# Softmax sums of the first batch moved from TensorE to GpSimd and VectorE, weight tiles moved by SyncE's queue, opening loads on two queues

## The chip, the cores and the metric

The kernel runs on one core of one Trainium2 chip. The metric is the device time of one launch in microseconds, as the median of the runs shown. A core has TensorE (PE in the profile; its weight loads are PEld), VectorE (DVE), ScalarE (ACT), GpSimd (POOL) and SyncE (SP), each with a queue of its own that it works off in order, and 16 DMA engines that all queues share. Matrix products land in PSUM, everything else lives in SBUF.

## The reference

The input x has 4 batches of 512 rows of 512. Post-norm attention with 16 query heads of 32 and a single key and value head, then a gated feed-forward part whose weights are quantized to -1, 0 and 1.

```python
q = rotary((x @ Wq + bq) split into 16 heads of 32)
k = rotary(x @ Wk + bk); v = x @ Wv + bv          # one head, shared by all
attn = softmax(q k^T / sqrt(32), axis=-1)
x = layernorm(x + (attn v) @ Wo + bo)

quantize(w) = clip(round(w / (mean(abs(w)) + 1e-8)), -1, 1)
h = sigmoid(x @ quantize(w1).T) * (x @ quantize(w2).T)   # 512 -> 1408
out = layernorm(x + h @ quantize(w3).T)
```

All data are float32. w1, w2 and w3 have 1408 x 512 elements each.

## The kernel before

**Steps.** The heads are handled in 4 chunks c of 4 heads (4 x 32 partitions), the keys in 4 tiles t of 128. The main loop runs over 64 steps (b, c, t); here step 0 to step 15 are batch 0. In step n the kernel issues, in this order on each engine: `scores` (products `ps`, in two PSUM pairs j of two heads each, less the row maxima `negm` by a product with ones; then two exponentials `es` of 128 x 1024 on ScalarE); `weigh` of the step before (products `acc` of `es` and v); `find_maxima` for step n + 7 (products `pmax`, again two pairs, and two maxima reductions `mx` on VectorE); one `quantize` job; some filler work; another `quantize` job in batch 0; and twice, in the middle and at its end, `due()`, which counts a slot and runs one piece of each entry in `late` whose slot has come.

**PSUM.** The pool `ps_sc` has two buffers of two banks, tag `sc`. `ps` and `pmax` take turns in them, so `pmax` waits for the exponentials of the same step, and the `ps` of the next step waits for the maxima of this one. `acc` and `den` have one bank each, and `ps_mm` two banks for the filler.

**Filler.** `project_in` makes k, v and the queries of a batch (`pk`, `pq`, then a rotation on VectorE of four operations: `a`, a shuffle, one with `sin_sb`, the addition; if it runs before step 0, ScalarE first copies the product to `r`). `project_out` and `feed_forward` follow for batches that are done. `fill.draw(pace)` takes so many microseconds of it in a step by lengths written into the code. In batch 0 the filler is the projection of batches 1 and 2.

**Maxima.** After the fourth `t` of a chunk, `spread` transposes the maxima on PE (`pm`, between the two groups of `pmax`), makes two rows of them (`m`), and sends them by SyncE to DRAM (`rows`) and back (`negm`). For batches 1 to 3 the queries are split in two parts (`halves`: a copy on ScalarE, a subtraction on GpSimd), stored (`qw`, `qp`) and loaded per head (`qr`), three steps ahead. From step 9 on, `pmax` is of that kind (kr, qr).

**Softmax sums.** In batch 0, `count` multiplies each `es` by ones on PE into the PSUM tile `den` (4 products of 512 columns, each in two passes). At the end of a chunk `normalize` copies `den` to SBUF on ScalarE, sends one row of every four heads to DRAM and back as 128 x 16 (`few`), takes the reciprocal, and loads it spread over the partitions (`rden`); GpSimd multiplies `ctxT` by it. In batches 1 to 3 GpSimd adds the `es` of the four t into `total` (four additions of 128 x 512 a step from t = 1 on), and `normalize` reduces `total` on VectorE with 32 x 32 transposes (`part`, two instructions), goes through DRAM (`parts`) to a `few` of 32 x 4 x 64, and reduces, inverts and transposes that (three instructions).

**Quantizing.** `quantized` works in 66 jobs: 33 first passes (ScalarE sums absolute values, `junk`) and 33 second ones (ScalarE's `sgn`, VectorE's `raw`, then a store to DRAM as `w`). A raw tile is loaded four jobs ahead into one of nine buffers and stored two jobs after it is done. In `now > PER` (after step 16) `sgn` is put in PSUM, before that in SBUF. Both transfers are issued by GpSimd:

```python
pool.dma_start(out=raws[k], in_=wf[m, f])       # load(k), line 178
pool.dma_start(out=w.bitcast(F32), in_=q)       # the store, line 218
```

All other transfers go through `move`, line 83, on SyncE, in the order in which the program issues them.

**Opening.** SyncE loads `bkv`, `bq`, `wkv`, the four x-transposed tiles of batch 0 (`xT`), and then the query weights and rotary tables. PE meanwhile runs 24 products of ones (`WARM`, 48 passes of 128 columns), then `pk`, which needs `wkv` and the four `xT`. Before step 0 the kernel finds the maxima of steps 0 to 6.

Helpers record all engine instructions under line 75, products under 80, transposes on PE under 86 and SyncE's transfers under 83, so the profile is read by tile names.

Of the kernel before, what the change touches and what calls it, by code (L numbers as in the profile page):

```python
# [28 lines left out]
def postln_block(  # L29
# [20 lines left out]
    NG = P // HD  # L50
    SCALE = 1.0 / float(HD) ** 0.5
    W = 512
    WARM = 24

    const = ctx.enter_context(tc.tile_pool(name="const", bufs=1))
    small = ctx.enter_context(tc.tile_pool(name="small", bufs=2))
# [25 lines left out]
    def move(out, in_):  # L82
        pin(nc.sync.dma_start(out=out, in_=in_))  # L83
# [34 lines left out]

    chunks = iter([(b, c) for b in range(B) for c in range(NC)])

    def load_xT(n):

        for _ in range(n):
            b, c = next(chunks, (None, None))
            if b is not None:
                batches[b].xT.append(work.tile([P, T], F32, tag="xT", name="xT", bufs=6))
                move(batches[b].xT[c], xT[b, :, c, :])

    move(bkv_sb, bkv)
    move(bq_sb, bq)  # L130
    move(wkv_sb, wkv)
    load_xT(NC)
    move(wq_sb[0], wq[:, 0])
    move(cos_sb, cos)
    move(sin_sb, sin)
# [22 lines left out]
    def quantized():  # L158

        order = ((0, False), (1, False), (0, True), (2, False), (1, True), (2, True))
        jobs = [(m, last, f) for m, last in order for f in range(NF)]

        means = {}
        for n, (m, last) in enumerate(order):
            if not last:
                for k, step in ((2, 0), (6, 1), (10, 2)):
                    means[(n + 1) * NF + k] = (m, step)
        raws, part, row, pg, hi, waiting = {}, {}, {}, {}, {}, []  # L170

        def load(k):
            if k < len(jobs):
                m, _, f = jobs[k]

                tag, bufs = ("wd", 5) if k % 2 else ("wg", 4)
                raws[k] = wp.tile([P, W], F32, tag=tag, name="raw", bufs=bufs)
                pool.dma_start(out=raws[k], in_=wf[m, f])

        def mean(m, step):  # L180
            if step == 0:
                row[m] = small.tile([P, 1], F32, tag="row", name="row")
                dve.tensor_reduce(row[m], part[m], AX.X, ALU.add)
            elif step == 1:
                pg[m] = ps_mm.tile([P, 1], F32, tag="mm", name="pg")
                mm(pg[m], ones, row[m], True, True)
                gamma = small.tile([P, 1], F32, tag="gamma", name="gamma")
                act.activation(gamma, pg[m], AF.Identity, scale=1.0 / (NF * W * P), bias=eps_q)
                row[m] = gamma
            else:  # L190
                hi[m] = small.tile([P, 1], F32, tag="hi", name="hi")
                act.mul(hi[m], row[m], 0.5)

        AHEAD = 4
        for k in range(AHEAD):
            load(k)
        for k, (m, last, f) in enumerate(jobs):
            load(k + AHEAD)
            if k in means:
                mean(*means[k])  # L200
            raw = raws.pop(k)
            if not last:
                if f == 0:
                    part[m] = small.tile([P, NF], F32, tag="part", name="part", bufs=3)
                junk = work.tile([P, W], BF16, tag="th", name="junk")
                act.activation(junk, raw, AF.Abs, accum_out=part[m][:, f : f + 1])
            else:
                if now > PER:

                    sgn = ps_acc.tile([P, W], F32, tag="den", name="sgn")  # L210
                else:
                    sgn = work.tile([P, W], BF16, tag="th", name="sgn")
                act.activation(sgn, raw, AF.Sign, bias=hi[m])
                dve.scalar_tensor_tensor(raw, raw, hi[m], sgn, ALU.is_gt, ALU.min)
                waiting.append((kept[m][f], raw))
            if len(waiting) > 2 or k + 1 == len(jobs):
                for w, q in waiting[: 1 if k + 1 < len(jobs) else 3]:
                    pool.dma_start(out=w.bitcast(F32), in_=q)
                del waiting[:1]
            yield  # L220

# [182 lines left out]
    def scores(b, c, t):  # L404
        s = batches[b]
        pss = []
        for j in range(2):
            ps = ps_sc.tile([P, 2, T], F32, tag="sc", name="ps")
            pss.append(ps)
            for i in range(2):  # L410
                rows = ts(2 * j + i, HD)
                mm(ps[:, i, :], s.kT[rows, ts(t, P)], s.q[c][rows, :], True, False)
        for j, ps in enumerate(pss):
            for i in range(2):
                rows = slice(HD * (2 * j + i), HD * (2 * j + i) + 2)
                mm(ps[:, i, :], ones_r[rows, :], s.negm[c][rows, :], False, True)
        es = []
        for j, ps in enumerate(pss):
            e = esp.tile([P, 2, T], F32, tag="es", name="es")
            act.activation(e, ps, AF.Exp, scale=SCALE)  # L420
            es.append(e)
        if b > 0:

            if t == 0:
                s.first = es
            elif t == 1:
                s.total = [work.tile([P, 2, T], F32, tag=f"total{j}", name="total", bufs=1) for j in range(2)]
                for j in range(2):
                    for i in range(2):
                        pool.tensor_tensor(  # L430
                            s.total[j][:, i, :], s.first[j][:, i, :], es[j][:, i, :], ALU.add
                        )
            else:
                for j in range(2):
                    for i in range(2):
                        pool.tensor_tensor(
                            s.total[j][:, i, :], s.total[j][:, i, :], es[j][:, i, :], ALU.add
                        )
        return es

    def columns(out, left, right, start, stop):
# [9 lines left out]
        if t == NT - 1:  # L451
            act.copy(s.ctxT[c], s.acc)

    def count(b, c, t, es):

        s = batches[b]
        if t == 0:
            s.den = ps_acc.tile([P, T], F32, tag="den", name="den")
        columns(s.den, ones[:, 0:HD], es, t == 0, t == NT - 1)

    def normalize(b, c):

        s = batches[b]
        flat = dram.tile([NG, T], F32, tag="flat1", name="flat", bufs=3)
        if b > 0:

            n = T // HD
            part = work.tile([P, NG * n], F32, tag="sums", name="part", bufs=1)
            for j in range(2):
                dve.tensor_reduce(  # L470
                    part[:, ts(j, 2 * n)],
                    s.total[j].rearrange("p i (a r) -> p (i a) r", r=HD),
                    AX.X, ALU.add, apply_transpose=True,
                )
                if j == 0 and c + 1 < NC:
                    yield
            yield
            parts = dram.tile([P // HD, HD, NG * n], F32, tag="parts", name="parts", bufs=3)
            move(parts.rearrange("o r k -> (o r) k"), part)
            yield  # L480
            few = work.tile([HD, P // HD + 2, NG * n], F32, tag="rot_b", name="few", bufs=1)
            move(few[:, 0 : P // HD, :], parts.rearrange("o r k -> r o k"))
            yield
            if c + 1 < NC:
                yield
            whole, lines = few[:, P // HD, :], few[:, P // HD + 1, :]
            dve.tensor_reduce(whole, few[:, 0 : P // HD, :].rearrange("r o k -> r k o"), AX.X, ALU.add)
            dve.reciprocal(whole, whole)
            dve.transpose(lines, whole)
            move(  # L490
                flat.rearrange("(b h) (a r) -> (h a) b r", b=2, r=HD),
                lines.rearrange("x (b r) -> x b r", b=2),
            )
        else:
            sums = work.tile([P, T], F32, tag="sums", name="sums", bufs=1)
            act.copy(sums, s.den)
            yield
            sent = dram.tile([NG, T], F32, tag="flat0", name="sent", bufs=3)
            move(sent, sums.rearrange("(i r) k -> i r k", r=HD)[:, 0])
            yield  # L500
            few = small.tile([P, NG * T // P], F32, tag="few", name="few")
            move(few, sent.rearrange("i (r j) -> (i r) j", r=HD))
            yield

            if c + 1 < NC:
                yield
            dve.reciprocal(few, few)
            move(flat.rearrange("i (r j) -> (i r) j", r=HD), few)
        yield
        rden = work.tile([P, T], F32, tag="rden", name="rden", bufs=1)  # L510
        for i in range(NG):
# [343 lines left out]
    for n, (b, c, t) in enumerate(steps):  # L855
# [4 lines left out]
        es = scores(b, c, t)  # L860
        if last is not None:
            weigh(*last)
        if last is not None and last[0] == 0:
            count(*last)
        last = (b, c, t, es)
        if n == NC * NT // 2:

            late.append((slot, load_x(0)))
        if t == NT - 1:
            begin = slot + 3  # L870
            late.append((begin, normalize(b, c)))
            if c == NC - 1:
                late.append((begin + 7, feed(b)))
# [91 lines left out]
```

## Time and profile before

| | us |
|---|---|
| runs | 670.32, 671.13, 673.02 (median 671.13) |
| profiled execution | 672.56 |
| its span, from the first to the last instruction | 670.8 |
| PE / VectorE / ScalarE / GpSimd busy | 644.7 / 430.0 / 282.8 / 324.4 |
| start of the first product `pk` | 9.77 |
| first `ps`, step 0 | 48.2 |
| batch 0, to its last `pq` | 48.2 to 161.3 |

The profile is that of one execution. "Busy" of PE counts overlapping passes once and includes passes that wait, so it is no measure of work. Views used below: the page (busy times, 40 slices of the span with a digit for the busy tenths, the chain of waits, groups of instructions), the stretches (busy time of every engine between two times), the answer for one tile, and the timeline (start, duration, engine, line, operation, out<-in, shape, count, and in brackets the idle time before it and what ended it). A line of the timeline with a count merges neighbours.

### The profile page before, as it was taken

The page shows a single profiled execution, that of the slowest core. Times are in us where ns is not written, and L with a number is a line of the kernel's source. Part 1 is how long each engine was busy: PE and PEld are TensorE (multiplying, and loading weights), DVE is VectorE, ACT ScalarE, POOL GpSimd, SP SyncE. Part 2 cuts the span into 40 slices and gives each one's busy share as a digit, 9 for nine tenths or more (in the row PEclk, how much of TensorE's full clock was granted, in tenths as well). Part 3 has the DMA queues.
Part 4 walks back from the last instruction along what each step waited for, and adds up shares of the span by engine and source line. Part 5 has one row for each costly group of instructions (what it writes and reads, how often), then busy time and mean ns, then how long its engine had stood idle before and what let it go on. Part 6 is the DMA issues. An engine that isn't in the chain of part 4 may idle for free.

```text
span 670.8 us, 9406 instructions
## 1 busy us (share of the span) xinstructions
PE 644.7 (96%) x3222; PEld 358.5 (53%) x3222; DVE 430.0 (64%) x619; ACT 282.8 (42%) x441; POOL 324.4 (48%) x414
## 2 busy tenths in 40 slices
PE   9989999999999989999999899999999999999995
PEld 6333333443333355665456466654555685778884
DVE  1896766587787867766666966676635553464335
ACT  1466555655443644333334445233435421234213
POOL 0615334535987776376666375576574802202000
PEclk9999999999999999999999999999999999999998
DMA  8755668688575286355132456351232364236531
GB/s 283 248 192 175 205 199 261 186 286 276 162 245 172 92 259 202 116 169 162 54 84 82 125 164 215 124 172 29 73 100 67 126 217 148 79 109 213 183 107 63
DMA packets 60671, 107.78 MB, mean 161 GB/s; under 512 B 14592, under 2 KB 15360, under 8 KB 60624
## 3 DMA queue, kind: packets, MB, share of 16 engines
q1 hardware_dynamic: 52560, 81.10, 38.5%
q0 software_dynamic: 7920, 25.96, 11.8%
q8 instruction: 25, 0.41, 0.3%
q14 instruction: 22, 0.18, 0.1%
q10 hardware_dynamic: 144, 0.13, 0.1%
HBM read 84.06 MB, written 23.10 MB: 160 GB/s over the span
## 4 chain that ended last, share of the span: by engine, by line
PE 81%; DVE 9%; DMA 4%; ACT 3%; issue 2%; SPq 1%; POOL 0%; DVEq 0%; ACTq 0%; POOLq 0%
PE gu L80 23%; PE po L80 19%; PE ps L80 11%; PE pmax L80 8%; PE acc L80 7%; PE pq L80 7%; DVE mx L75 3%; PE den L80 2%; DMA wg<-w 2%; ACT es L75 2%; PE pk L80 1%; DVE xt L75 1%; PE warm L80 1%; SPq L83 1%; DMA xT<-in_xT 1%
## 5 line engine op out<-in xcount | busy, mean ns | idle before, releaser
L75 DVE TENSOR_REDUCE mx<-pmax 128x1 f32<-128x512 f32 (+1 forms) x159 | 158.1, 1007 | 81.3 <-PE pmax L80 81.1
L75 ACT ACTIVATE es<-ps 128x1024 f32<-128x1024 f32 x128 | 124.2, 1022 | 141.9 <-PE ps L80 133.9
L80 PE MATMUL gu<-y,wg 128*128 128x512 f32 x704 | 172.9, 395 | 2.0 <-DMA wg<-w 1.1
L80 PEld LDWEIGHTS gu<-y,wg 128*128 128x128 f32 x704 | 131.1, 188 | 38.4 <-issue 4.7
L75 POOL TENSOR_TENSOR total<-total,es 128x512 f32<-128x512 f32 x96 | 123.8, 1319 | 45.2 <-ACT es L75 45.1
L80 PE MATMUL po<-wd,h 128*128 128x512 f32 x352 | 87.0, 395 | 4.2 <-DVE y L75 2.9
L75 POOL TENSOR_TENSOR total<-es 128x512 f32<-128x512 f32 x48 | 60.5, 1290 | 55.8 <-ACT es L75 55.8
L80 PE MATMUL pmax<-kr,qr 128*128 128x512 f32 x192 | 75.2, 455 | 3.7 <-ACT es L75 2.2
L80 PEld LDWEIGHTS po<-wd,h 128*128 128x128 f32 x352 | 64.9, 188 | 22.5 <-DVE y L75 4.6
L75 ACT CAST h<-hw 128x512 fp32r<-128x512 f32 x44 | 27.3, 620 | 100.7 <-DVE hw L75 100.7
L80 PE MATMUL acc<-es,v 128*32 128x512 f32 x512 | 68.2, 605 | 0.0
L80 PEld LDWEIGHTS pmax<-kr,qr 128*128 128x128 f32 x192 | 33.6, 188 | 57.0 <-ACT es L75 20.9
L75 DVE SCALAR_TENSOR_TENSOR hw<-th,gu 128x512 f32<-128x512 f32 x44 | 30.2, 687 | 46.9 <-PE gu L80 46.8
L80 PE MATMUL po<-wo_sb,ctxT 128*128 128x512 f32 x128 | 58.9, 593 | 0.3 <-DVE hw L75 0.3
L80 PE MATMUL ps<-negm,ones_r 2*128 2x512 f32 x256 | 58.2, 788 | 0.0
L75 DVE SCALAR_TENSOR_TENSOR xt<-po,xt 128x512 f32<-128x512 f32 x48 | 32.8, 684 | 38.1 <-PE po L80 38.1
L75 DVE TENSOR_TENSOR h<-hw,h 128x512 fp32r<-128x512 f32 x44 | 42.1, 957 | 21.7 <-ACT h L75 21.4
L80 PE MATMUL ps<-qT,kT 32*128 32x512 f32 x384 | 55.6, 640 | 0.0
L75 POOL DMA_DIRECT2D raw<-in_wf x66 | 36.1, 549 | 37.4 <-DMA w<-raw 26.7
L80 PE MATMUL pq<-xT,wq_sb 128*128 128x512 f32 x112 | 53.0, 601 | 1.0 <-ACT v L75 1.0
L75 ACT ACTIVATE th<-gu 128x512 f32<-128x512 f32 x44 | 26.3, 598 | 49.1 <-PE gu L80 49.0
L80 PEld LDWEIGHTS po<-wo_sb,ctxT 128*128 128x128 f32 x128 | 24.1, 189 | 22.0 <-issue 19.2
(98 smaller groups left out, 639.2 us busy)
## 6 DMA issues: line engine op xcount, KB each, us to landing
wg<-w SPq DMA_DIRECT2D x88, 256.0 KB
raw<-in_wf POOLq DMA_DIRECT2D x66, 256.0 KB, 4.6
qr<-qp SPq DMA_DIRECT2D x96, 128.0 KB
wd<-w SPq DMA_DIRECT2D x44, 256.0 KB
w<-raw POOLq DMA_DIRECT2D x33, 256.0 KB, 4.9
qp<-q SPq DMA_DIRECT2D x48, 128.0 KB
rden<-flat SPq DMA_DIRECT2D x64, 64.0 KB
xt<-in_x SPq DMA_DIRECT2D x16, 256.0 KB
```

Of the source, the lines that this page charges most:

```text
L75: return lambda *args, **kw: pin(getattr(self.engine, name)(*args, **kw))
L80: pin(nc.tensor.matmul(out, lhsT=lhsT, rhs=rhs, start=start, stop=stop))
L83: pin(nc.sync.dma_start(out=out, in_=in_))
```

## The change

Six things change. `count`, `den` and the batch-0 branch of `normalize` go, and batch 0 takes the way of the others: GpSimd's additions, then `part` and `few` on VectorE. In batch 0 `normalize` begins four slots after the chunk's last step (at the end of the next step) and not three, and does its two `part` reductions in one piece. The loads and stores of the tiles to be quantized are issued by SyncE. At the opening, SyncE and ScalarE issue the four `xT` in turns, ScalarE then the two bias tiles, and SyncE starts with `wkv`. `WARM` is 10.

```diff
-    WARM = 24
+    WARM = 10
...
-    def load_xT(n):
+    def load_xT(n, engines=(nc.sync,)):
...
-                move(batches[b].xT[c], xT[b, :, c, :])
-
-    move(bkv_sb, bkv)
-    move(bq_sb, bq)
+                pin(engines[k % len(engines)].dma_start(out=batches[b].xT[c], in_=xT[b, :, c, :]))
+
     move(wkv_sb, wkv)
-    load_xT(NC)
+    load_xT(NC, (nc.scalar, nc.sync))
+    pin(nc.scalar.dma_start(out=bkv_sb, in_=bkv))
+    pin(nc.scalar.dma_start(out=bq_sb, in_=bq))
...
-                pool.dma_start(out=raws[k], in_=wf[m, f])
+                move(raws[k], wf[m, f])
...
-                    pool.dma_start(out=w.bitcast(F32), in_=q)
+                    move(w.bitcast(F32), q)
...
-        if b > 0:
-
-            if t == 0:
-                s.first = es
-            elif t == 1:
...
+        if t == 0:
+            s.first = es
+        elif t == 1:
+            s.total = [work.tile([P, 2, T], F32, tag=f"total{j}", name="total", bufs=1) for j in range(2)]
+            for j in range(2):
+                for i in range(2):
+                    pool.tensor_tensor(
+                        s.total[j][:, i, :], s.first[j][:, i, :], es[j][:, i, :], ALU.add
+                    )
...
-    def count(b, c, t, es):
-
-        s = batches[b]
-        if t == 0:
-            s.den = ps_acc.tile([P, T], F32, tag="den", name="den")
-        columns(s.den, ones[:, 0:HD], es, t == 0, t == NT - 1)
-
     def normalize(b, c):
...
-                if j == 0 and c + 1 < NC:
-                    yield
+            if j == 0 and b > 0 and c + 1 < NC:
+                yield
...
-        else:
-            sums = work.tile([P, T], F32, tag="sums", name="sums", bufs=1)
-            act.copy(sums, s.den)
...
-            dve.reciprocal(few, few)
-            move(flat.rearrange("i (r j) -> (i r) j", r=HD), few)
...
-        if last is not None and last[0] == 0:
-            count(*last)
...
-            begin = slot + 3
+            begin = slot + (4 if b == 0 else 3)
```

More of the change, by code (lines that the diff above doesn't have):

```diff
@@ L119, in postln_block @@
     chunks = iter([(b, c) for b in range(B) for c in range(NC)])
-    def load_xT(n):
-        for _ in range(n):
+    def load_xT(n, engines=(nc.sync,)):
+        for k in range(n):
             b, c = next(chunks, (None, None))
@@ L421, in scores @@
             es.append(e)
-        if b > 0:
-            if t == 0:
-                s.first = es
-            elif t == 1:
[L427 to L432, printed above, removed]
-            else:
[L434 to L438, printed above, removed]
+        if t == 0:
[7 more added lines that the diff above has]
+                    )
+        else:
+            for j in range(2):
+                for i in range(2):
+                    pool.tensor_tensor(
+                        s.total[j][:, i, :], s.total[j][:, i, :], es[j][:, i, :], ALU.add
+                    )
         return es
@@ L464, in normalize @@
         flat = dram.tile([NG, T], F32, tag="flat1", name="flat", bufs=3)
[L465 to L474, printed above, removed]
-                if j == 0 and c + 1 < NC:
-                    yield
-            yield
[L478 to L494, printed above, removed]
-            sums = work.tile([P, T], F32, tag="sums", name="sums", bufs=1)
-            act.copy(sums, s.den)
[L497 to L506, printed above, removed]
-            dve.reciprocal(few, few)
-            move(flat.rearrange("i (r j) -> (i r) j", r=HD), few)
@@ new lines, in normalize @@
+        n = T // HD
+        part = work.tile([P, NG * n], F32, tag="sums", name="part", bufs=1)
+        for j in range(2):
+            dve.tensor_reduce(
+                part[:, ts(j, 2 * n)],
+                s.total[j].rearrange("p i (a r) -> p (i a) r", r=HD),
+                AX.X, ALU.add, apply_transpose=True,
+            )
+            if j == 0 and b > 0 and c + 1 < NC:
+                yield
+        yield
+        parts = dram.tile([P // HD, HD, NG * n], F32, tag="parts", name="parts", bufs=3)
@@ new lines, in normalize @@
+        move(parts.rearrange("o r k -> (o r) k"), part)
+        yield
+        few = work.tile([HD, P // HD + 2, NG * n], F32, tag="rot_b", name="few", bufs=1)
+        move(few[:, 0 : P // HD, :], parts.rearrange("o r k -> r o k"))
+        yield
+        if c + 1 < NC:
+            yield
+        whole, lines = few[:, P // HD, :], few[:, P // HD + 1, :]
+        dve.tensor_reduce(whole, few[:, 0 : P // HD, :].rearrange("r o k -> r k o"), AX.X, ALU.add)
+        dve.reciprocal(whole, whole)
+        dve.transpose(lines, whole)
@@ L509, in normalize @@
+        move(
+            flat.rearrange("(b h) (a r) -> (h a) b r", b=2, r=HD),
+            lines.rearrange("x (b r) -> x b r", b=2),
+        )
         yield
```

## Prediction

> **What bounds the kernel now.** First the page's busy times and the slices (of 16.8 us each): TensorE (PE) is busy everywhere, so a gain has to shorten its chain.
>
> ```profile
> PE 644.7 (96%) x3222; PEld 358.5 (53%) x3222; DVE 430.0 (64%) x619; ACT 282.8 (42%) x441; POOL 324.4 (48%) x414
> ...
> DVE  1896766587787867766666966676635553464335
> ```
>
> PE's 96% counts passes that wait inside; VectorE (DVE) is far from idle in the first batch, slices 3 to 9. Second, the stretches and the tile that goes away:
>
> ```profile
> 48.20:161.30 113.10, 112.14 (x650) 43.12 (x650) 78.89 (x109) 66.04 (x111) 51.18 (x72) 1.00 0.68 219
> ...
> L80 PE MATMUL den<-es,ones x128: 592/592/593, 57.0 to 157.9; 128*32 128x512 f32 x128
> ```
>
> Columns of the first: stretch, length, then busy us of PE, PEld, DVE, ACT, POOL, clock, DMA share, GB/s. The 128 passes of den fill 16.7 us by the groups view. Third, the timeline: a step of batch 0 that still has den, then a step of batch 1 that has none.
>
> ```profile
> 70.12 1.94 ACT L75 ACTIVATE es<-ps 128x1024 f32<-128x1024 f32 x2 [3.38 <-PE ps L80]
> 70.22 1.06 PE L80 MATMUL acc<-es,v 128*32 128x512 f32 x8
> 71.11 1.04 PE L80 MATMUL den<-es,ones 128*32 128x512 f32 x8
> 72.08 1.16 PE L80 MATMUL pmax<-kT,room 32*128 32x512 f32 x8
> 73.25 2.36 DVE L75 TENSOR_REDUCE mx<-pmax 128x2 f32<-128x1024 f32 x2 [0.26 <-PE pmax L80]
> ...
> 172.63 1.07 PE L80 MATMUL acc<-es,v 128*32 128x512 f32 x8
> 172.73 1.94 ACT L75 ACTIVATE es<-ps 128x1024 f32<-128x1024 f32 x2 [2.33 <-PE ps L80]
> 173.80 0.30 PEld L80 LDWEIGHTS pmax<-kr,qr 128*128 128x128 f32 x2 [1.02 <-ACT es L75]
> ```
>
> What to see: call T the start of acc. With den, pmax starts at T+1.86; without it, at T+1.18, because then ScalarE's first exponential, which frees the PSUM pair, is late. So 16.7 us of products are worth 0.68 a step, not 1.04. And batch 0 is a ring through VectorE: ps and pmax share two PSUM pairs, so the next scores wait for this step's second maximum. Maxima end to next T: 75.61 to 76.96 is 1.35 (82.35 to 83.69 gives 1.34). Ring with den: 3.03 (T to first maximum) + 2.36 + 1.34 = 6.73, just the distance of T from 70.22 to 76.96. Steps 9 on use kr,qr for pmax: 2.62 + 2.36 + 1.34 = 6.32.
>
> **The change, part by part.**
>
> *Products.* Ring without den: 6.05, and 5.65 from step 9; there PE's own queue needs 2.67 + 1.90 (pq) + 1.31 (ps) = 5.88. Steps 1 and 5, which transpose maxima between two pmax groups, go from 7.40 to 6.72. All light steps win 0.4 to 0.7.
>
> *VectorE's added sums.* The rows are in batch 1:
>
> ```profile
> 209.92 0.58 DVE L75 TENSOR_REDUCE few<-few 32x64 f32<-32x256 f32 x1
> 210.54 0.54 DVE L75 RECIPROCAL few<-few 32x64 f32<-32x64 f32 x1
> 211.11 0.23 DVE L75 STREAM_TRANSPOSE few<-few 32x64 f32<-32x64 f32 x1
> ...
> 226.96 1.24 DVE L75 TRANSPOSE_TENSOR_REDUCE part<-total 128x32 f32<-128x1024 f32 x1
> ```
>
> Two part reductions at 1.16 start to start are 2.32 a chunk, the few group 1.42, less a reciprocal of 0.16: 3.58 x 4 = 14.3 us. The order of the changed kernel puts part at the end of steps 4, 8, 12 and 16, and few at the end of 6, 10 and 14 (and in 18), ahead of the next maxima. Queued behind them are those maxima, and PE waits for them. A step (first maximum to first maximum) is thus the longer of the ring and 2.27 + VectorE's other work, in start-to-start times: raw 0.66, a rotation 2.85 (that of kT 3.68), m 0.20.
>
> - Step 4: 2.27 + 0.66 + 2.85 + 0.66 + 2.32 = 8.76. Step 8: 2.27 + 0.29 (wait for kv) + 3.68 + 2.32 = 8.56. Step 12, with the 0.15 of row: 8.91.
> - Step 6: 2.27 + 2.85 + 1.42 = 6.54. Step 10, which waits 0.35 for pq: 6.89. Step 14: 2.27 + 0.66 + 2.85 + 0.66 + 1.42 = 7.86. Step 2: 6.44.
> - Others: step 0, 6.60; 1, 6.72; 3 and 7, 6.05; 5 (ring and m), 6.25; 9 and 13, 5.85; 11 and 15, 5.65.
>
> Sum over steps 0 to 15: 25.81 + 27.60 + 26.95 + 28.27 = 108.6. Now the first maximum of step 0 starts at 51.86 and that of step 16 at 159.16: 107.3. So batch 0 costs **+1.3**: light steps give back about 11, the heavy ones take it. Step 16's part is covered by the 3.5 us of projection in that step, and few in 18 likewise; were that cover gone, up to 2.3 + 1.4. Bounds: -10.9 (16 x 0.68, VectorE never late) to +1.3 plus the contention below.
>
> *GpSimd.* 48 additions at 1.27 are 61 us; with its q, kr, ctxT and xt steps (17 x 1.27) and one kT of 1.77, 84 of 109 us. Additions start at T+1.2 and take 5.0; with a q step behind, done by T+7.5. Part is asked for at about the next T+9, so 7 us later; es has six buffers, two a step (one lent to spare at first), and the additions release them before the third step. No cost. The four ScalarE copies of den (2.5 us) were off the path: nothing.
>
> *Transfers to SyncE.* 66 loads and 33 stores leave GpSimd (0.549 each, 54 us) and take some 0.43 each on SyncE. There a load into a buffer waits until its last store has landed, 6.2 us after issue (76.97 to 83.19). Behind it stand rows, negm, parts, few, qw, qp, qr, rden and xT. A store is issued two jobs, one step, ahead, so the wait left is about 0 to 1 us; negm has two steps of slack, qr three, few about 6 us (part ends at the end of step 4, few is used at the end of 6). Only xT in step 16 has none: PE waits 0.5 there now. Value 0, bounds -1 (less issue on GpSimd) to +4 (four chunks late by 1 us each).
>
> *Opening.* Rows:
>
> ```profile
> 1.64 0.42 SPq L83 DMA_DIRECT2D wkv_sb<-in_wkv  x1
> ...
> 9.77 3.60 PE L80 MATMUL pk<-xT,wkv_sb 128*128 128x512 f32 x8
> ...
> 4.00:5.00 1.00, 1.00 (x7) 1.00 (x6) 0.00 (x0) 0.00 (x0) 0.00 (x0) 1.00 0.86 162
> ...
> 8.00:9.00 1.00, 1.00 (x12) 1.00 (x11) 0.00 (x0) 0.00 (x0) 0.00 (x0) 1.00 1.05 354
> ```
>
> pk starts where the 48 warming passes end, with no wait for data. With 20 passes (2, 7, 6, 7 in the first slices) they end at about 4.75. The five tiles (1.31 MB) landed at about 8.2 by the GB/s summed; wkv is issued 0.91 earlier and two tiles go by ScalarE's queue, so at about 7.3 or before. Passes run at 7 a us before, 12 after about 7.2 us, though the granted clock reads 1.00. Take pk's passes at 0.86 until 7.2 (2.85 of them), then 0.43 (5.15): end 9.41 + 0.16 = 9.57 against 13.37. **-3.8**; -1.6 if all eight are slow (11.8), -5.0 if none is. The sixth pass ends at 8.55, behind the last tile's 7.3. What follows (VectorE 25.1 of 26.8 us busy up to 48.2) has its data in time and just moves; ScalarE's four issues (1.7 us) end before it is needed.
>
> The Trainium skill, "TensorE: Matmul & The Clock Gate", Part 1: PE runs at half rate until it has been busy for a window of about 3.4 us that does not start with the kernel. A shorter warming of 3.2 us may by that rule miss its window, which speaks against this part; the sum by it would be the -1.6 above.
>
> Sum: 672.56 (the profiled execution: span 670.8 and 1.8 around it) - 3.8 + 1.3 = 670.1; the median of the runs is 1.43 lower: **668.6**.
>
> **Rivals.**
>
> *PE sets the pace* (VectorE's extra hides in its 31 idle us of batch 0): every step wins 0.68. 671.1 - 3.8 - 10.9 = 656.4. For: den in the chain, 2%. Against: VectorE's idle time lies ahead of pmax, where it has nothing it may run first.
>
> *Slower: VectorE's quantizing operation and GpSimd's additions want the same port.* The rows that show it are batch 1's:
>
> ```profile
> 252.19 0.65 DVE L75 TENSOR_TENSOR h<-hw,h 128x512 fp32r<-128x512 f32 x1
> ...
> 265.90 1.73 DVE L75 TENSOR_TENSOR h<-hw,h 128x512 fp32r<-128x512 f32 x1
> ...
> 262.04 5.04 POOL L75 TENSOR_TENSOR total<-total,es 128x512 f32<-128x512 f32 x4 [2.81 <-ACT es L75]
> ```
>
> The same operation, two SBUF inputs, takes 0.65 with GpSimd idle and 1.73 while it adds. In batch 0 raw reads raw and sgn, both in SBUF (sgn moves to PSUM only after step 16). Six of its 20 runs there are on the path: two in step 2, the second in 4 and 12, two in 14. At 1.08 each +6.5: 675.1. It decides from 0.98 each (3.36 above 671.1). At half an addition (0.63), +3.8: 672.4. Against: part of them fall between additions.
>
> The Trainium skill, "SBUF — State Buffer", Who interferes with whom: VectorE with two SBUF inputs and GpSimd reading SBUF exclude each other for a whole instruction. By it the wait is what is left of a 1.27 addition, so the sum would lie between 668.6 and 676.2.
>
> *SyncE's queue is late:* a load's 6.2 us wait falls ahead of few or xT and VectorE or PE stands. Four chunks at 1 to 2 us: 673 to 677. For: one queue now carries all; against: the slacks above.
>
> *The change does less than it says:* den is gone from the instruction order, so only the opening can fail: 670.8.
>
> **How the numbers follow.** Forecast 0.48, around 668.6, its own range 665 to 672.5 (opening -1.6 to -5.0, one to two us of contention): half of it is faster by over 0.5% (3.4 us, about what a measurement of this kernel can tell), half within. PE's pace 0.22, mostly as a part of its 10.9: 656 to 664. Port 0.20: 672.4 to 676. Queue 0.10: 673 to 677. Range 658 to 677: it leaves out the lowest part of PE's pace (0.06) and about 0.06 above. Faster 0.24 + 0.21 = 0.45; within 0.22 + 0.01 + 0.03 + 0.02 = 0.28; slower 0.02 + 0.17 + 0.08 = 0.27.
>
> **What would show it.** Right: pk ends near 9.6; pmax starts at T+1.2 in batch 0; steps 4, 8 and 12 take 8.5 to 9, light ones about 6; VectorE over 90 us busy in batch 0; first maxima of steps 0 and 16 about 108.6 apart. Wrong: raw over 1.2 on average, or long waits of VectorE for few (slower); part steps under 7 (faster); pk with all passes at 0.86.

## The result, and the profile after

The changed kernel takes 682.66 us (median of 6 runs, 678.14 to 685.28); the kernel before, run beside it, 672.55 (670.32 to 674.25). The ratio is 1.015 [1.012, 1.018]: slower by 1.5%, where 668.6 and a gain were forecast. The profiled execution is the shortest of the six, 678.14 us with a span of 676.4; before it was 672.56 and 670.8. So the trace shows 5.6 us of a loss of 10, and the experiments have to give the rest.

From the page of the kernel after, the busy times and two rows of the slices (16.9 us each); PEclk is the granted TensorE clock in tenths:

```profile
PE 642.6 (95%) x3066; PEld 353.8 (52%) x3066; DVE 450.4 (67%) x635; ACT 281.0 (42%) x437; POOL 337.9 (50%) x363
...
DVE  2988976887897776776676866566635453455435
PEclk9999999977999999999999999999999999999998
```

TensorE has 156 instructions fewer and is not done sooner. New is the clock: 0.7 in slices 9 and 10, the end of batch 0. The stretch of batch 0 after, taken from as far ahead of step 0's first maximum to as far behind that of step 16 as the row of before (columns as there):

```profile
44.66:166.88 122.22, 113.19 (x519) 41.12 (x519) 95.81 (x121) 64.19 (x107) 88.81 (x65) 0.93 0.65 199
```

It is 9.1 us longer (122.22 against 113.10), VectorE has 16.9 us more work in it, and the clock is 0.93, not 1.00. The opening, from the timeline:

```profile
5.91 3.92 PE L80 MATMUL pk<-xT,wkv_sb 128*128 128x512 f32 x8
```

pk ends at 9.83, 3.54 earlier than before, and the first maximum of step 0 starts 3.54 earlier, at 48.32. That of step 16 comes at 164.74, 5.58 later than before. So the opening gains 3.5 and batch 0 loses 9.1. Steps 16 and 17 lose 1.4 more (the 18th acc starts 6.96 later than before), which the rest of the kernel makes up: the span ends 5.6 later.

Where batch 0 loses it: VectorE's timeline at the end of step 12, then TensorE's behind it.

```profile
137.63 0.74 DVE L75 SCALAR_TENSOR_TENSOR raw<-raw,hi,sgn 128x512 f32<-128x512 f32 x1
138.29 2.37 DVE L75 TRANSPOSE_TENSOR_REDUCE part<-total 128x32 f32<-128x1024 f32 x2
140.57 1.19 DVE L75 TENSOR_REDUCE mx<-pmax 128x2 f32<-128x1024 f32 x1
...
143.00 2.59 DVE L75 SCALAR_TENSOR_TENSOR raw<-raw,hi,sgn 128x512 f32<-128x512 f32 x2
```

```profile
137.69 1.98 PE L80 MATMUL pq<-xT,wq_sb 128*128 128x512 f32 x4 [0.40 <-DVE q L75]
141.82 1.13 PE L80 MATMUL ps<-room,kT 32*128 32x512 f32 x4 [2.14 <-DVE mx L75]
...
145.56 1.94 PE L80 MATMUL acc<-es,v 128*32 128x512 f32 x8
147.42 2.08 PE L80 MATMUL pmax<-kr,qr 128*128 128x512 f32 x4
```

part, and a raw of 1.88 us earlier in the step, delay the maxima, the next scores wait 2.14 us for them, and then the same products that took 1.07 (acc) take 1.94. The clock in the stretches around this wait, and around a second one of 1.07 us at 157.44:

```profile
140.00:143.00 3.00, 1.13 (x4) 0.30 (x4) 3.00 (x4) 0.00 (x0) 3.00 (x3) 1.00 0.20 66
143.00:150.00 7.00, 6.87 (x21) 2.87 (x22) 3.91 (x5) 2.54 (x3) 7.00 (x6) 0.51 1.00 326
...
157.00:160.00 3.00, 1.93 (x10) 0.60 (x10) 2.97 (x5) 0.00 (x0) 3.00 (x4) 1.00 0.43 137
160.00:167.00 7.00, 7.00 (x22) 2.71 (x17) 3.17 (x4) 3.14 (x4) 3.31 (x2) 0.51 0.87 287
```

A wait of one or two us is followed by about seven us at half clock. A third fall, of half that length, follows the wait of 1.53 us for step 10's scores. Last, what SyncE's queue waited for from 48 to 182 us, the row of before and then the row of after (in total, times, longest):

```profile
SPq L83 <- POOL q L75: 1.6, 1, 1.6
```

```profile
SPq L83 <- POOL q L75: 12.2, 4, 4.0
```

GpSimd's low halves of q now stand behind its additions, and SyncE's stores of them hold up what is queued behind. All 12.2 us lie before 140 us; whether anything on the path comes of them, this trace does not say.

### The profile page after: what moved, and what is told of

It is laid out like the page before. It is cut to its first block, busy times and chain, and to the rows that moved or that the text cites. A ratio compares the mean times of both kernels' runs of the same rounds, so it can differ in the third digit from the quotient of the medians.

```text
span 676.4 us, 9162 instructions
## 1 busy us (share of the span) xinstructions
PE 642.6 (95%) x3066; PEld 353.8 (52%) x3066; DVE 450.4 (67%) x635; ACT 281.0 (42%) x437; POOL 337.9 (50%) x363
## 4 chain that ended last, share of the span: by engine, by line
PE 73%; DVE 12%; DMA 5%; ACT 4%; SPq 3%; issue 2%; POOL 0%; DVEq 0%; ACTq 0%; POOLq 0%
PE gu L80 23%; PE po L80 18%; PE ps L80 10%; PE pmax L80 8%; PE acc L80 6%; PE pq L80 5%; DVE mx L75 4%; ACT es L75 3%; SPq L83 3%; DVE part L75 2%; PE pk L80 1%; DVE xt L75 1%; DMA rows<-m 1%; DMA qr<-qp 1%; DMA xT<-in_xT 1%
## 5 line engine op out<-in xcount | busy, mean ns | idle before, releaser
L75 POOL TENSOR_TENSOR total<-total,es 128x512 f32<-128x512 f32 x128 | 165.5, 1325 | 55.9 <-ACT es L75 55.9
L75 POOL TENSOR_TENSOR total<-es 128x512 f32<-128x512 f32 x64 | 83.0, 1327 | 77.4 <-ACT es L75 57.3
L80 PE MATMUL pmax<-kr,qr 128*128 128x512 f32 x192 | 78.8, 471 | 5.1 <-ACT es L75 3.7
L80 PE MATMUL acc<-es,v 128*32 128x512 f32 x512 | 70.6, 624 | 0.0
L80 PE MATMUL ps<-qT,kT 32*128 32x512 f32 x384 | 57.2, 642 | 1.1 <-DVE mx L75 1.1
L80 PE MATMUL pq<-xT,wq_sb 128*128 128x512 f32 x112 | 54.4, 615 | 1.5 <-ACT v L75 1.0
L75 DVE TRANSPOSE_TENSOR_REDUCE part<-total 128x32 f32<-128x1024 f32 x32 | 38.7, 1227 | 0.0
```

The source lines that it names most:

```text
L75: return lambda *args, **kw: pin(getattr(self.engine, name)(*args, **kw))
L80: pin(nc.tensor.matmul(out, lhsT=lhsT, rhs=rhs, start=start, stop=stop))
```

## The experiments

Each ratio is to runs of the kernel before on the same chip, whose medians lie between 671.98 and 672.55, so that times of different groups of runs can be set side by side to about half a us. "The change" is the kernel after; steps are counted by acc: the n-th acc belongs to step n.

**The opening alone.** Edit, on the kernel before: the opening of the diff (`WARM = 10`, `load_xT` on two queues, the biases by ScalarE).

> The kernel before with the changed opening alone (10 warming products, the tiles of x by two queues). My theory (the opening is worth its 3.5 us, and the loss lies in batch 0, where VectorE's lateness lets TensorE idle and its granted clock then falls to half): pk ends near 9.8, first maxima of steps 0 and 16 stay 107.3 apart, granted clock 0.99 or more, 669 us (ratio 0.995). Rival (the shorter warming is what brings the later falls of the clock): clock under 0.99, stretches at half rate in batch 0, 673 us or more.

Measured: 669.51 us, ratio 0.995 [0.993, 0.997], clock 0.997, none of the 5 us stretches from 45 to 195 us under 1.00. The opening is good for what was forecast, and the shorter warming is not what brings the falls.

**One operand of raw in PSUM.** Edit, on the change:

```
-                if now > PER:
+                if now >= 0:
                     sgn = ps_acc.tile([P, W], F32, tag="den", name="sgn")
```

> The changed kernel with sgn in the free PSUM bank from the main loop's start, so that raw reads one operand in SBUF, not two. Port contention as a large part of the cause: raw goes from 1.08 on average to 0.7, of the 6.9 us that this frees about half lies on the path, TensorE's waits for mx become shorter and fewer falls of the clock follow; 116.4 between the first maxima of steps 0 and 16 becomes 108 to 112, granted clock 0.99, 674 to 678 us. Rival (VectorE's two part reductions alone make the waits; the port is marginal): the same falls of the clock, 680 to 683 us. Rival (SyncE's queue): unchanged, 682 us.

Measured: 680.70 us, ratio 1.013 [1.009, 1.016]; the time missed, though raw did what was said. Groups of raw of the change (48 to 165 us) and of this kernel (48 to 170), with min, median and max in ns:

```profile
L75 DVE SCALAR_TENSOR_TENSOR raw<-raw,hi,sgn x20: 719/922/1878, 54.0 to 160.2; 128x512 f32<-128x512 f32 x20
```

```profile
L75 DVE SCALAR_TENSOR_TENSOR raw<-raw,hi,sgn x22: 715/740/748, 55.2 to 169.4; 128x512 f32<-128x512 f32 x22
```

The 17th acc starts at 164.47, 6.5 us before that of the change (171.00), and no stretch of batch 0 from 55 us on is under 1.00. But the 18th starts 16.8 us later, not 8.6, with the clock at 0.50 from 172 to 178 us.

**TensorE's waits filled.** Edit, on the change:

```
+        if n in (6, 10, 14, 16):
+            idle = ps_acc.tile([P, P], F32, tag="den", name="idle")
+            for _ in range(6):
+                mm(idle, ones, ones, True, True)
         es = scores(b, c, t)
```

> The changed kernel with six products of ones (128 columns, no data waited for, result unused) in TensorE's queue ahead of the scores of steps 6, 10, 14 and 16, where TensorE waited for VectorE. VectorE's work is as it was. My theory (the idle time brings the clock down, and most of the 5.6 us lost in steps 12 to 15 is the half rate after it): clock 0.99 or more, no stretch at 0.50, steps 13 to 15 at 6 to 7 us, 676 to 678 us. Rival (the waits themselves are the loss and the half rate is hidden beside VectorE's work): the clock is up but the time is 681 to 684 us. Rival (the falls come from something else than the idle time): clock 0.98 as before, 682 us or a little more.

Measured: 681.54 us, 1.014 [1.011, 1.016]. The time lies in the range of the first rival (681 to 684 us), but the trace does not bear that rival out: again batch 0 is faster (17th acc at 164.60, one fall of 3 us is left, from 143 to 146), again the 18th comes late, 17.6 us after. TensorE's timeline there says why, and SyncE's queue ahead of it:

```profile
174.18 3.86 PE L80 MATMUL pk<-xT,wkv_sb 128*128 128x512 f32 x4 [6.69 <-DMA xT<-in_xT]
```

```profile
163.80 3.15 SPq L83 DMA_DIRECT2D qp<-q  x4
167.05 1.09 SPq L83 DMA_DIRECT2D qr<-qp  x2
168.18 0.58 SPq L83 DMA_DIRECT2D raw<-in_wf  x1
168.87 0.38 SPq L83 DMA_DIRECT2D w<-raw  x1
169.34 0.88 SPq L127 DMA_DIRECT2D xT<-in_xT  x2
```

The last two tiles of x are issued at 169.3, at 168.9 in the change, and at 161.3 in the kernel before. TensorE reaches the work that needs them at 167.5 here and stands 6.69 us. From 171 to 180 us its clock is at 0.50, so that pk then takes 3.86 us and not 1.88. In the profiled execution of the change it was late itself, and waited 0.52. So there are two losses, and each covers the other: curing one shows the other.

**The tiles to be quantized by GpSimd again.** Edit, on the change: `pool.dma_start(...)` for the two `move` of raw and w.

> The changed kernel with the tiles to be quantized loaded and stored by GpSimd again, not SyncE. My theory (SyncE's queue is not what is late): within 0.5 per cent of the changed kernel, 680 to 685 us; if anything slower, since 46 issues at 0.54 add 25 us to a GpSimd that has 84 of 109 us taken in batch 0. Rival (SyncE's queue delays rows, few, qr or xT): 673 to 677 us.

Measured: 697.51 us, 1.040 [1.035, 1.045], far outside what I had said. A load of raw stands 4.79 us on GpSimd for a store to land, as such loads did before (5.41 us at 137.8); but now the additions stand behind it. SyncE's queue waits for the low halves of q more than twice as long as in the change:

```profile
SPq L83 <- POOL q L75: 30.0, 6, 7.5
```

So the move to SyncE saves the sums' change some 15 us. The pair belongs together.

**The last tiles of x by ScalarE.** Edit, on the change:

```
-        load_xT(NC if b == 0 else 2)
+        load_xT(NC if b == 0 else 2, (nc.scalar,) if b == 2 else (nc.sync,))
```

> The changed kernel with the last batch's last two tiles of x loaded by ScalarE's queue instead of SyncE's; nothing else. Revised theory (two losses that cover each other: VectorE's lateness in steps 12 to 15 with the half clock after it, and SyncE's queue, which issues these tiles at 169 us whatever TensorE does, so that TensorE stands up to 7 us for them in step 17): the tiles are issued at about 165, the wait in step 17 stays under 2.5 us, the second loss goes and the first stays, 676 to 679 us. Rival (the late tiles are only a sign; SyncE's queue is late for qr and negm too, and TensorE stands for those next): 681 to 684 us.

Measured: 676.93 us, 1.007 [1.004, 1.009], 5.7 under the change. The tiles are issued at 161.8 (165 expected), and pk in step 17 has no wait:

```profile
171.37 1.88 PE L80 MATMUL pk<-xT,wkv_sb 128*128 128x512 f32 x4
```

In this trace SyncE's queue passes the place where these loads stood at 171.7. With the 4.8 us from their issue to pk in the trace above (169.34 to 174.18), TensorE would have had them at 176.5, 5.1 us after it asked. That is an estimate; the 5.7 itself rests on the medians, because the two profiled executions differ in batch 0 already (115.76 us from the 1st to the 17th acc here, 118.44 in the change).

**Both cures, twice.** The same edit with sgn in PSUM, and with the waits filled.

> The changed kernel with both cures: sgn in PSUM in batch 0, and the last two tiles of x by ScalarE's queue. Revised theory (losses that cover each other): neither cure alone gained more than 2 us, the two together gain 7 to 9: the 17th acc starts at about 164.5, as with sgn in PSUM alone, step 17 takes 8.4 to 11, 672 to 675 us. Rival (a third thing waits behind them, such as qr): over 678 us.

> The changed kernel with TensorE's waits filled by products of ones (result unused) ahead of the scores of steps 6, 10, 14 and 16, and the last two tiles of x by ScalarE's queue. Revised theory: as with sgn in PSUM, 672 to 676 us; the 17th acc at about 164.6 and step 17 at 8.4 to 11. If the half clock is a large part of the first loss, it comes out below the same kernel without the filling by 3 to 6 us; if it is not, within 2 us of it.

Measured: 673.42 us, 1.002 [1.000, 1.005], and 673.40, 1.003 [1.000, 1.006]. Each gains 3.5 us more on top of 5.7 by the medians of ten runs (2.6 and 2.8 by the means), where sgn in PSUM by itself had gained 2.0 and the filling 1.1, neither clear of the spread of the runs. Step 17 takes 7.56 us in both, less than expected. The filling takes nothing off VectorE (raw still reaches 1.88 us), so what it gains is what TensorE's idle time costs beyond itself, through the clock: with x by ScalarE alone the trace has two falls, of 3.4 and 6.8 us, with the filling too only the first. The shorter raw gains the same 3.5, and its trace also has a single fall of 3.4 us. The two were not tried together, so how far it is the same time is open.

**The products back.** Edit, on the kernel before: the opening and SyncE's moving of the tiles, without the sums' change.

> The changed kernel with the sums of batch 0 by products of ones again, as in the kernel before: the opening and SyncE's moving of the tiles remain. My theory (SyncE's queue is late in step 16 only because GpSimd's additions hold up the low halves of q, for which SyncE's stores stand, and because parts and few are waited for there): without the additions the tiles of x are issued no more than 2 us later than in the kernel before, 668 to 671 us, as with the opening alone. Rival (66 loads and 33 stores are by themselves too much for SyncE's queue): the wait for xT is there too, 675 us or more.

Measured: 670.38 us, 0.997 [0.995, 0.999], near the opening alone. The wait for x is 0.17:

```profile
163.56 2.18 PE L80 MATMUL pk<-xT,wkv_sb 128*128 128x512 f32 x4 [0.17 <-DMA xT<-in_xT]
```

99 transfers more are not by themselves what makes SyncE's queue late; that needs the sums' change with them. What in the sums' change does it is open. I expected GpSimd's low halves of q. But in the change and in the kernel with the waits filled every wait of SyncE's queue for them lies before 140 us. From 157 us on, ahead of the tiles of x, the queue waits for the sums and next to nothing else; the change, then the kernel with the waits filled:

```profile
SPq L83 <- DVE few L75: 2.0, 1, 2.0
```

```profile
SPq L83 <- DMA flat<-few: 2.3, 1, 2.3
```

From there to xT it issues almost without a pause, for 11.5 and 9.8 us. VectorE is done with few at 157.35 in the change, at 147.68 in the kernel before, since the new order puts it at the end of step 14 and not between the maxima of that step. That speaks for the place of the sums in the queue and against the low halves of q; no run tests either by itself.

**The sums two slots earlier.** What was left was part and few, which stand in steps with a rotation. Edit, on the change:

```
-            begin = slot + (4 if b == 0 else 3)
+            begin = slot + (2 if b == 0 else 3)
...
-                late.append((begin + 7, feed(b)))
+                late.append((begin + (9 if b == 0 else 7), feed(b)))
```

alone; with the x tiles by ScalarE; and with sgn in PSUM too.

> The changed kernel with the sums of batch 0 begun two slots earlier: part at the end of steps 3, 7, 11 and 15, few at the end of 5, 9 and 13, which hold no rotation, instead of the steps after them, which do; the same instructions otherwise. Theory (VectorE is late only where part or few meets a rotation; a step without one has 2.27 + 1.32 + 2.32 = 5.91 us of work, under its ring of 6.05): steps 4, 8 and 12 fall by about 2 us each, step 14 by 1, few falls of the clock are left; the wait for xT in step 17 stays as long as SyncE's queue is late, 672 to 678 us. Rival (the sums cost VectorE their length wherever they stand): 681 to 684 us. Rival (at the end of a step the additions of that step are not done, and VectorE stands for them): over 684 us.

> The same, and the last two tiles of x by ScalarE's queue. Theory: no wait for xT over 2.5 us is left; about 7 us below the kernel with ScalarE's queue alone (676.9), 666 to 671 us. Rival (the sums cost their length wherever they stand): 676 to 678 us.

> The same, with sgn in PSUM in batch 0 as well. Theory: VectorE on time in every step but the one with kT's rotation, 16 steps of batch 0 at 6.3 on average; 663 to 668 us, under the kernel before (672.5) and under the opening alone (669.5). Rival: 672 to 674 us, as without the earlier sums.

Measured: 678.23 us (1.010 [1.006, 1.015]), 677.52 (1.009 [1.006, 1.012]) and 676.62 (1.006 [1.004, 1.009]). All three miss what was expected, the first by 0.2 us (it is 4.4 us under the change, and its wait for xT is 3.89 us, not gone). The steps fell as said: from the 5th to the 6th acc 6.78 us in the third kernel, after 8.55 with part in the later place; from the 9th to the 10th 6.99 after 9.25. But two new waits took more than that, in VectorE's timeline of the third kernel:

```profile
125.89 1.25 DVE L75 TRANSPOSE_TENSOR_REDUCE part<-total 128x32 f32<-128x1024 f32 x1 [4.41 <-POOL total L75]
128.33 1.25 DVE L75 TRANSPOSE_TENSOR_REDUCE part<-total 128x32 f32<-128x1024 f32 x1 [1.20 <-POOL total L75]
...
171.06 0.57 DVE L75 TENSOR_REDUCE few<-few 32x64 f32<-32x256 f32 x1 [6.57 <-DMA few<-parts]
```

In chunk 2 GpSimd had additions of xt ahead of those of total; in chunk 3 few has one slot less, and SyncE, late with its queue, issued the store of parts only at 165.59 and the load of few at 168.39, though part was done at 156.8.

**The sums placed.** Edit, on the kernel with both cures (ScalarE's tiles, sgn in PSUM):

```
-        if n == NC * NT // 2:
+        if n == 11:
...
-            begin = slot + (4 if b == 0 else 3)
+            begin = slot + (3 if b > 0 else 2 if c + 1 < NC else 4)
```

> The changed kernel with sgn in PSUM in batch 0, the last two tiles of x by ScalarE's queue, the sums of chunks 0 to 2 two slots earlier, those of chunk 3 where the change has them, and the four loads and additions of xt begun at step 11, not 8. Theory (the two waits that the earlier sums brought, 4.4 + 1.2 us of VectorE for total behind three additions of xt and 6.6 us for few, go; the gain in steps 4, 8, 12 and 14 stays): step 12 at 6 to 8 us, step 17 at 7.6 to 9, 663 to 668 us, under the kernel before (672.0) and under the opening alone (669.5). Rival (a further wait takes their place, such as that for rden or xt): 670 us or more.

Measured: 666.82 us (664.16 to 670.52), ratio 0.993 [0.990, 0.995]: faster than the kernel before, and than the change by 15.8 us. It is 2.7 us under the opening alone (669.51), but the two intervals overlap, so a gain from the sums' change itself is likely and not shown. The edit moves the sums and xt at once; which of the two does how much was not tried. In VectorE's timeline part now stands at the end of step 3, and the next maxima are late by next to nothing:

```profile
71.85 0.75 DVE L75 SCALAR_TENSOR_TENSOR raw<-raw,hi,sgn 128x512 f32<-128x512 f32 x1 [0.80 <-ACT sgn L75]
72.51 2.36 DVE L75 TRANSPOSE_TENSOR_REDUCE part<-total 128x32 f32<-128x1024 f32 x2
74.80 2.32 DVE L75 TENSOR_REDUCE mx<-pmax 128x2 f32<-128x1024 f32 x2
```

From the 1st to the 17th acc it takes 104.71 us, the kernel before 108.16 and the change 118.44. The longest wait of TensorE for mx in batch 0 is 0.57 us, and one fall of the clock is left behind it (0.50 from 144 to 146).

## Why the prediction was wrong, point by point

- *Opening*: right. -3.5 for -3.8; passes at 0.49 us on average, between the two rates assumed. The rule on the warming (3.2 us may miss its window) did not bite.
- *The ring and VectorE's sums*: right in kind, and nearly in size where its assumptions held. In the kernel with both cures (sgn in PSUM, x by ScalarE) the 16 steps sum to 111.3 us (first maximum of step 0 at 48.55, of step 16 at 159.85) where the hand sum has 108.6. Steps 4 and 12 take 8.72 and 8.81 (8.76 and 8.91 by hand). Off by most are step 8 (9.41, not 8.56: VectorE waited 1.16 us for kv, not 0.29), step 14 (9.19, not 7.86: few waited 1.29 us for its load) and step 15 (6.59, not 5.65, in the one fall of the clock).
- *Port (VectorE's raw beside GpSimd's additions), taken at 0*: the first step that failed. raw is 1.08 us on average in batch 0 after (21.4 us for 20), 0.74 before; one operand in PSUM brings it back. Worth 3.5 us of the median. That this is about the +3.8 of the rival's lower price is partly luck: the rival added up raw's own extra time, and the filling gets the same 3.5 without touching raw. The section "Who interferes with whom" of the Trainium skill's "SBUF — State Buffer" says that one SBUF input frees VectorE from GpSimd; the 22 runs of raw at 715 to 748 ns agree.
- *Transfers, taken at 0*: the second that failed, and the largest: 5.7 us of the median. I looked for the wait at a load of raw, and gave few 6 us of slack for its own use, without asking what waits behind it in SyncE's queue. xT, whose slack I had called none (the wait of 0.5 that I put in step 16 reads 0.38 before, in step 17), was issued 7.6 us later than before, and TensorE stood 6.1 and 6.7 us for it in the two kernels that reached it on time. That it takes the sums' change is shown, and that another queue cures it; what in the sums' change makes the queue late is open, and the traces point to few. The rival of a late queue named the right tile and was priced at 10%; the waits it named, of a load for a store to land, are there too (5.6 us in two, the last over at 141.3), but not next to xT.
- *GpSimd, "no cost"*: not shown either way by a run of its own. I counted its busy time and the buffers of es, not who waits behind its additions. After, SyncE stands 12.2 us for its low halves of q (1.6 before), and GpSimd itself stands for part (7.89 us from 74.5), since total has one buffer.
- *Clock*: in no step, the third that failed. I had TensorE at 1.00 after as before, and took a wait at its own length. In the profiled execution steps 0 to 15 sum to 116.4 us for the 108.6 by hand; of these 7.8, steps 9, 13 and 15, in which the falls begin, have 5.0 (6.74, 8.11 and 7.46 for 5.85, 5.85 and 5.65). Of the median, filling the waits gave 3.5, the same as the shorter raw, and not to be added to it.

The sum, by medians: 682.66, less 5.7 (x by ScalarE), less 3.5 (raw, or the idle time filled), gives 673.4; the forecast was 668.6. Of the 4.8 left, 2.7 are the sum of batch 0's steps (111.3 for 108.6), 0.3 is the opening, and 1.4 is the base: I took 671.13, the median of three runs of the kernel before, where the six beside the change give 672.55. 0.4 is not accounted for. Why the other five runs of the change were up to 7 us longer than the profiled one is argued only: they have no trace, and the late x tiles fit.

## What to carry to other kernels

Work that moves to an engine with idle time is paid by where in the step it stands: the same part reductions cost 2 us at the end of a step that has a rotation, and next to nothing at the end of one that has none. When an in-order queue is given more to wait for, list what stands behind each wait, also on the queues that wait for that engine in turn. And when a cure shows up in its own stage and not in the total, look for a second loss behind it before dropping the theory.

## What the runs showed of the hardware

The granted clock fell to half after waits of TensorE far shorter than I had thought: 2.14 and 1.07 us in the change, each time for about seven us (0.51 from 143 to 150 and from 160 to 167), and 1.53 us, for about 3.4. It does not always: a wait of 1.53 us at the same scores (step 10) was followed by no fall in three of the other kernels, nor were waits of 1.62 and 1.08 with sgn in PSUM. And in the last kernel a fall came after a wait of 0.57. So the length of one wait does not decide it. The Trainium skill, "TensorE: Matmul & The Clock Gate", HAM oscillation, has the rule as no idle gaps over some 3.4 us; here falls came after gaps of a third of that and less, and the measurement decides. The page's free-running window would fit that the same gap falls once and not another time; no run here tests it.
